# Four mask steps of graph 0 and layer 1's to 3's weights, later in a recorded order

## The chip, the cores and the metric

The kernel runs on one core of a Trainium2 chip. The time is the device time of one execution in microseconds; below, "us" is microseconds. Engines are named as the profile names them: PE is TensorE (PEld its weight loads), DVE is VectorE, ACT is ScalarE, POOL is GpSimd, SP is the engine that issues most of the transfers.

## The reference

Sixteen graphs of 1024 nodes with 256 features each go through four layers. Every layer normalizes the features, takes the positive part and adds its own result to them.

```
x: (16, 1024, 256) f32, adj: (16, 1024, 1024) int32 of 0 and 1, symmetric, ones on the diagonal
for each layer:
    h = max(layernorm(x), 0)
    x = x + layer(h, adj)
layer 0:  Wh = h W; e = leaky_relu(f1_i + f2_j, 0.2), f = Wh a; softmax over axis 1 of e where adj > 0; elu(att Wh)
layer 1:  the same with softmax over the last axis
layer 2:  relu(h W_upd + mean over neighbours of h W_msg + bias)
layer 3:  4 heads of 64: edges by type (adj is 0 or 1, so one type), leaky_relu 0.01, softmax,
          relu(att Wh + bias) + Wh, layernorm with gamma and beta
```

The exponential of a leaky ReLU of a sum is the larger of two products of exponentials, so a 1024 x 1024 matrix of weights comes from one row (the same on all 128 partitions) and one number for each partition.

## The kernel before

A graph's 1024 nodes are eight tiles of 128 (index n, i or j). In layer 0 (`layer0`, L742) a graph goes through these stages:

- *Projection* (L744 to L748): for each of eight tiles, two matmuls into PSUM (`project`, L683, tile ps_proj) and one ACT copy to hs (L746). Then `m.step()` (L747).
- *Row* (L750): the column of one attention term is gathered (L717), transposed on PE (L699, ps_col), exponentiated twice on ACT (L703, e_row), written to DRAM (L705, d_row) and read back as a broadcast to all partitions (L711, row), 512 KB each; layer 0 needs two such rows.
- *j loop* (L766 to L783): for each j, `m.step(2)` while steps are left; DVE makes p from the rows (L769), multiplies it by the mask and sums it (L771), takes the reciprocal (L772); ACT scales hs by it (L773). PE multiplies p by hs for the two output tiles i=0 and i=1 (L759, the "early" tiles; two PSUM buffers).
- *i loop* (L786 to L796): output tiles i=2 to 7, sixteen L759 matmuls each; ACT makes e and v (L791, L793), DVE adds them to the features (L736, L737 in `residual`), after each second tile a shift (L635); ACT makes hn (L667) and a sum of squares (L640), and PE transposes hn (L680, `flip`) for the next layer.

Layer 1 (`layer1`, L798) has the same stages with one row, one DVE instruction for each p (L822) and matmuls at L815.

*Masks.* `Mask` (L548) turns the int32 adjacency into bytes in sixteen steps for a graph, two for each tile j. A step (L575) is an ACT instruction over 128x512 with a sum; it reads a tile raw, of which there are three buffers, and then issues the load of the next raw on SP (L566, 256 KB). Graph 0 has four steps among the statistics at its start (L1011), then one after each projection, and the rest in the j loop. `Mask(1)` issues graph 1's first three loads.

*Weights.* Layer 0's are loaded first. `more()` (L1037) makes the others: `weights01` (L495) loads wx, wts and avs and makes two further columns of wx with PE (L507, ps_wa) and four DVE copies (L511); `weights2` (L513) loads two matrices and four rows (each broadcast to 128 partitions, 128 KB), and adds -2 to row_beta on DVE (L521); `weights3` (L523) loads wx, w3ts and a3s and makes eight columns with eight small products (L534) and sixteen DVE copies (L535, L536). a3s shares its two buffers (tag "e") with the tile e of L791. Each load is held back by a one-element copy (`behind`, L482) that reads the last p tile recorded so far, which makes the load wait until that p is written. The loads of later graphs' features (xs, L545, POOL) and of layer 2's adjacency (adj, L585, POOL) are held back in the same way.

*Order.* All graphs are generators. A queue sorted by a running time (L1050) takes the one that is due, lets it record instructions up to its next `yield`, and adds the yielded number to its time. Graphs start 120 apart. A scheduler then orders each engine's instructions from what was recorded; instructions passed to `later` (all of SP's loads among them) keep the recorded order. Graph 0's j loop is recorded at 26.6 to 47.4, its i loop from 47.4 to 78.6 and layer 1's projections from 80.9.

Of the kernel before, what the change touches and what calls it, by code (L numbers as in the profile page):

```python
# [421 lines left out]
def tile_simple_stack(  # L422
# [12 lines left out]
    B, N, D = x.shape  # L435
# [77 lines left out]
    def weights2():  # L513
        wx[2] = t = load_w(w2_msg, D, "wx2", 2 * D)
        later(nc.sync.dma_start(t[:, :, D:], w2_upd.rearrange("(c p) f -> p c f", p=P)))
        for name, src in (("bias2", bias2), ("bias3", bias3), ("gamma3", gamma3), ("beta3", beta3)):
            rows[name] = const.tile([P, D], F32, name=f"row_{name}")
            behind(rows[name][:1, :1])
            later(nc.sync.dma_start(rows[name], src.partition_broadcast(P)))

        nc.vector.tensor_scalar(rows["beta3"], rows["beta3"], -2.0, None, op0=OP.add)  # L521
# [16 lines left out]
    def load_x(b):  # L538
        t = state.tile([P, NT, D], F32, tag="xs", name="xs", bufs=3)
        if 0 < b < 3:  # L540
            behind(t[:1, 0, :1])
            behind(t[:1, PER, :1])
        for g in range(NHALF):
            part = slice(g * PER, (g + 1) * PER)
            nc.gpsimd.dma_start(t[:, part, :], x[b, g * HALF : (g + 1) * HALF].rearrange("(n p) d -> p n d", p=P))  # L545
        return t
# [136 lines left out]
    def project(norm, w, n, width):  # L683
        ps = mm_ps.tile([P, HALF], F32, tag="mm", name="ps_proj")
        for c in range(DC):
            nc.tensor.matmul(ps[:, :width], norm.ht[:, c, n * P : (n + 1) * P], w[:, c, :width], start=(c == 0), stop=(c == DC - 1))  # L686
        return ps

    def new_hs(name="hs"):
        return state.tile([P, NT, W3], F32, tag="hs", name=name, bufs=3)  # L690

    def spread(col, n, scales, name):

        k = n * NT
        ps = tr_ps.tile([P, P], F32, tag="tr", name="ps_col")
        nc.tensor.transpose(ps[:k, :], col, ident)  # L699
        all_rows = []  # L700
        for scale in scales:
            e = small.tile([H * NT, P], F32, tag="e_row", name="e_row", bufs=2)
            nc.scalar.activation(e[:k, :], ps[:k, :], AF.Exp, scale=scale)  # L703
            d = dram.tile([n, N], F32, tag=f"row_{name}", name="d_row", bufs=4)
            later(nc.sync.dma_start(d.rearrange("r (t p) -> (r t) p", p=P), e[:k, :]))  # L705
            all_rows += [d[r] for r in range(n)]
        return all_rows

    def everywhere(d, tag):
        row = work.tile([P, N], F32, tag=tag, name="row", bufs=2)  # L710
        later(nc.sync.dma_start(row, d.partition_broadcast(P)))  # L711
        return row

    def column(src, n):

        col = small.tile([P, H, NT], F32, tag="col", name="col", bufs=2)
        nc.vector.tensor_copy(col[:, :n, :], src.rearrange("p t n -> p n t"))  # L717
        return col[:, :n, :].rearrange("p n t -> p (n t)")

    def watch(b, layer, terms):  # L720
        k = b * 3 + layer
        nc.vector.tensor_reduce(top[:, k : k + 1], terms, axis=AX.XY, op=OP.max, apply_absolute_value=True)

    def weights(name):
        return work.tile([P, N], F32, tag="p", name=name, bufs=NT)

    def residual(xs, i, v, after, e=None):

        x = xs[:, i, :]
        if i % 2 == 0:  # L730
            if i == NT - 2:
                after.settle()
            after.flip()
            after.sums = small.tile([P, 2], F32, tag="sums", name="sums")
        if e is not None:
            nc.vector.scalar_tensor_tensor(x, e, 1.0, x, op0=OP.min, op1=OP.add)  # L736
        nc.vector.scalar_tensor_tensor(x, v, 0.0, x, op0=OP.max, op1=OP.add, accum_out=after.sums[:, i % 2 : i % 2 + 1])  # L737
        if i % 2:
            after.pair(xs, i // 2, after.sums)


    def layer0(b, xs, m, norm, after):  # L742
        hs = new_hs()
        for n in range(NT):  # L744
            ps = project(norm, wx[0], n, D + 2)
            nc.scalar.activation(hs[:, n, : D + 2], ps[:, : D + 2], AF.Copy, scale=norm.rs[n])  # L746
            m.step()  # L747
            yield 0.9  # L748
        mask = m.bytes
        row_a, row_b = [everywhere(d, "row") for d in spread(column(hs[:, :, D : D + 1], 1), 1, (1.0, S), "l0")]  # L750
        q = small.tile([P, NT], F32, tag="q", name="q")
        nc.scalar.activation(q, hs[:, :, D + 1], AF.Exp, scale=1.0 - S)
        watch(b, 0, hs[:, :, D : D + 2])
        yield 6.38
        ps_ = []
        early = [at_ps.tile([P, HALF], F32, tag="at", name="ps_o0") for _ in range(EARLY)]

        def product(ps, i, j):
            m = nc.tensor.matmul(  # L759
                ps[:, :D], ps_[j][:, i * P : (i + 1) * P], hs[:, j, :D], start=(j == 0), stop=(j == NT - 1)  # L760
            )
            if i < EARLY and j < 7:
                later(m)

        for j in range(NT):
            if m.raws:  # L766
                m.step(2)
            p = weights("p0")
            nc.vector.scalar_tensor_tensor(p, row_a, q[:, j : j + 1], row_b, op0=OP.mult, op1=OP.max)  # L769
            z = small.tile([P, 2], F32, tag="z", name="z", bufs=8)  # L770
            nc.vector.scalar_tensor_tensor(p, p, 1.0, mask[:, j, :], op0=OP.mult, op1=OP.mult, accum_out=z[:, 0:1])  # L771
            nc.vector.reciprocal(z[:, 1:2], z[:, 0:1])  # L772
            nc.scalar.activation(hs[:, j, :D], hs[:, j, :D], AF.Copy, scale=z[:, 1:2])  # L773
            ps_.append(p)
            if b == 0:
                gates.append(p)
            for i, ps in enumerate(early):
                if j:
                    product(ps, i, j - 1)
            yield 2.6  # L780
        for i, ps in enumerate(early):
            product(ps, i, NT - 1)
        for i in range(NT):  # L783
            if i < EARLY:
                ps = early[i]
            else:  # L786
                ps = at_ps.tile([P, HALF], F32, tag="at", name="ps_o0")
                for j in range(NT):
                    product(ps, i, j)
            e = work.tile([P, D], F32, tag="e", name="e")  # L790
            nc.scalar.activation(e, ps[:, :D], AF.Exp)  # L791
            v = work.tile([P, D], F32, tag="v", name="v")
            nc.scalar.copy(v, ps[:, :D])  # L793
            residual(xs, i, v, after, e)
            yield 3.9
# [49 lines left out]
    def degrees(b):  # L845

        t = small.tile([P, NT], F32, tag="deg", name="deg", bufs=2)
        halves = squares[:, b * NT * NHALF : (b + 1) * NT * NHALF].rearrange("p (n g) -> p n g", g=NHALF)
        nc.vector.tensor_tensor(t, halves[:, :, 0], halves[:, :, 1], op=OP.add)
        return t  # L850
# [155 lines left out]
    def graph(b):  # L1006
        xs = loaded.pop(b)
        m = masks.pop(b)
        norm = Norm()
        for g in range(NT // 2):  # L1010
            norm.pair(xs, g)  # L1011
            m.step()
            yield 2.66
        for layer, inputs in ((layer0, (m,)), (layer1, (m.bytes,)), (layer2, ())):
            yield 2.36
            norm.settle()
            norm.flip()
            after = Norm(degrees(b) if layer is layer1 else None)
            yield from layer(b, xs, *inputs, norm, after)
            norm = after  # L1020
        yield 1.44
        norm.flip()
        res = state.tile([P, NT, H, HW], F32, tag="res", name="res", bufs=1)
        hs = yield from layer3(b, xs, m.bytes, norm, res)
        return tail(b, xs, hs, res)
# [3 lines left out]
    def loads(b):  # L1029
        loaded[b] = load_x(b)  # L1030
        yield 30.0
        masks[b] = Mask(b)
        yield 0


    APART = 120.0
    def more():  # L1037

        weights01(1, w1, w1_t, a1, (1, 0))
        yield 21.6  # L1040
        weights2()
        yield 10.0
        weights3()
        yield 0
# [2 lines left out]
    next(loads_0)  # L1047
    weights01(0, w0, w0_t, a0, (0, 1), wait=False)
    next(loads_0)
    queue = [(32, 0, more())] + [(b * APART, b, graph(b)) for b in range(B)] + [(b * APART - 80, b, loads(b)) for b in range(1, B)]  # L1050
    while queue:
        queue.sort(key=lambda g: g[:2])
        at, b, g = queue.pop(0)
# [86 lines left out]
```

## Time and profile before

| | us |
|---|---|
| eight runs, median (lowest to highest) | 2619.87 (2618.07 to 2626.23) |
| the profiled execution: its time | 2620.04 |
| its span, first to last instruction | 2617.7 |
| first p of layer 0 (L769), graph 0 | 35.41 |
| last mask product of layer 0's j loop (L771) starts | 54.91 |
| layer 1's row is issued (L711) | 101.17 |
| first p of layer 1 (L822) | 105.65 |

The page's first rows give each engine's busy time and share of the span; its rows of digits cut the span into 40 slices of 65 us, with the busy share of each in tenths and the granted TensorE clock. The chain of waits follows the work that ended last backward, with the start and length of each piece in us. The timeline lists instructions in order: start, length, engine, line, operation, what it writes from what it reads, and in brackets the engine's idle time before and what ended it. "SPq" and "POOLq" rows are the issue of a transfer, not the transfer. The busy time of the engines in stretches of the first 120 us (from and to, length, then busy us and number of instructions for each engine, the mean granted clock, the share of the DMA engines and GB/s):

```
core 0: us, PE busy (x) PEld busy (x) DVE busy (x) ACT busy (x) POOL busy (x), PEclk, DMA share, GB/s
30.00:35.40 5.40, 0.00 (x0) 0.00 (x0) 0.00 (x0) 0.00 (x0) 0.00 (x0) 0.50 0.77 242
35.40:56.20 20.80, 10.87 (x29) 8.57 (x30) 19.92 (x41) 3.55 (x8) 1.57 (x2) 0.50 0.23 68
56.20:63.20 7.00, 6.70 (x31) 5.51 (x30) 4.09 (x27) 4.03 (x12) 4.79 (x6) 0.96 0.58 175
63.20:73.10 9.90, 9.90 (x50) 8.43 (x48) 2.95 (x11) 4.81 (x15) 1.70 (x3) 1.00 2.13 273
73.10:79.80 6.70, 4.70 (x20) 3.16 (x19) 1.34 (x12) 1.45 (x4) 0.00 (x0) 0.81 0.81 267
79.80:86.00 6.20, 6.20 (x22) 5.26 (x23) 1.38 (x8) 3.27 (x10) 0.00 (x0) 0.66 0.01 3
86.00:99.60 13.60, 12.53 (x58) 9.26 (x56) 2.13 (x9) 8.06 (x22) 1.21 (x2) 1.00 0.00 0
99.60:107.10 7.50, 0.05 (x2) 0.05 (x1) 1.45 (x2) 4.30 (x12) 0.00 (x0) 0.60 0.58 175
107.10:116.60 9.50, 9.46 (x32) 7.37 (x32) 8.38 (x9) 5.60 (x17) 0.00 (x0) 0.78 0.58 194
```

### The profile page before, as it was taken

The numbers are of one execution on the slowest core, as the hardware profiler recorded it, in microseconds if no ns is written. First come the engines' busy times: TensorE is split into PE (matmuls) and PEld (weight loads), VectorE is DVE, ScalarE is ACT, GpSimd is POOL, SyncE is SP. The second block draws the span as 40 slices with busy tenths as digits, with TensorE's granted clock in tenths as the row PEclk, the third lists the DMA queues.
The fourth block names the chain that finished last, engine by engine and source line by source line (L and its number), as shares of the span: only waits on it lengthen the run. The fifth ranks groups of instructions, "written<-read, shape, count | busy, mean of one in ns | idle before, by whom it ended". The sixth has DMA issues, their size and how long they took to land.

```text
span 2617.7 us, 62976 instructions
## 1 busy us (share of the span) xinstructions
PE 2472.8 (94%) x26194; PEld 2098.9 (80%) x26194; DVE 1965.8 (75%) x3815; ACT 1447.8 (55%) x4065; POOL 438.4 (17%) x454
## 2 busy tenths in 40 slices
PE   5899999999999999999999999999999999999985
PEld 4688788888878888788888878888888888878864
DVE  4357778787777977778787777877778787777858
ACT  4563755637565474755637565473755637565350
POOL 1010211203012030211203112030211203111021
PEclk7899999999999999999999999999999999999997
DMA  4541441616217261351616216161351616215021
GB/s 154 116 85 54 104 99 58 126 63 141 70 44 151 67 125 55 96 108 58 125 58 144 72 52 143 66 125 54 98 106 58 125 59 141 72 52 118 26 65 36
DMA packets 212633, 233.76 MB, mean 89 GB/s; under 512 B 10416, under 2 KB 161072, under 8 KB 212336
## 3 DMA queue, kind: packets, MB, share of 16 engines
q0 software_dynamic: 137728, 83.90, 19.3%
q1 hardware_dynamic: 74608, 145.73, 17.1%
q8 instruction: 208, 3.41, 0.5%
q14 instruction: 89, 0.73, 0.1%
HBM read 212.35 MB, written 17.24 MB: 88 GB/s over the span
## 4 chain that ended last, share of the span: by engine, by line
PE 51%; DVE 15%; ACT 14%; DMA 9%; issue 8%; POOL 2%; SPq 0%; DVEq 0%; POOLq 0%; ACTq 0%
PE ps_o L759 16%; PE ps_proj L686 11%; PE ps_o L942 11%; PE ps_o L883 6%; DVE p L929 5%; DVE p L822 5%; ACT hn L667 3%; DMA raw<-in_adj_t 3%; DMA row<-d_row 3%; ACT mask L575 3%; PE pt_h L680 2%; ACT unread L640 2%; PE ps_o L877 2%; PE ps_o L815 2%; POOL rs L593 2%
## 5 line engine op out<-in xcount | busy, mean ns | idle before, releaser
L929 DVE SCALAR_TENSOR_TENSOR p<-row,q,mask 128x1024 f32<-128x1024 f32 x512 | 633.2, 1279 | 61.5 <-PE ps_o L942 50.9
L942 PEld LDWEIGHTS ps_o<-hb,p 128*64 128x64 f32 x16384 | 506.2, 138 | 97.6 <-issue 45.3
L942 PE MATMUL ps_o<-hb,p 128*64 128x65 f32 x16384 | 544.7, 224 | 19.8 <-DVE p L929 6.2
L686 PE MATMUL ps_proj<-wx,ht 128*128 128x258 f32 (+2 forms) x2048 | 518.7, 392 | 6.4 <-ACT hs L746 5.0
L815 PE MATMUL ps_o<-hs,p 128*128 128x257 f32 x2048 | 498.6, 390 | 11.8 <-ACT mask L575 7.5
L759 PE MATMUL ps_o<-hs,p 128*128 128x256 f32 x2048 | 493.8, 386 | 16.5 <-ACT hs L773 16.2
L759 PEld LDWEIGHTS ps_o<-hs,p 128*128 128x128 f32 x2048 | 379.9, 192 | 69.6 <-ACT hs L773 20.7
L686 PEld LDWEIGHTS ps_proj<-wx,ht 128*128 128x128 f32 x2048 | 360.5, 190 | 86.2 <-ACT hs L746 16.0
L815 PEld LDWEIGHTS ps_o<-hs,p 128*128 128x128 f32 x2048 | 373.7, 191 | 68.3 <-ACT mask L575 8.0
L592 POOL TENSOR_SCALAR rs<-mv 128x4 f32<-128x4 f32 (+1 forms) x112 | 33.6, 300 | 1559.7 <-ACT unread L640 1545.0
L736 DVE SCALAR_TENSOR_TENSOR xs<-e,xs 128x256 f32<-128x256 f32 x256 | 108.2, 422 | 233.2 <-ACT e L791 162.4
L593 POOL TENSOR_TENSOR rs<-rs,neg_half 128x4 f32<-128x4 f32 (+2 forms) x144 | 257.3, 1790 | 10.7
L667 ACT ACTIVATE hn<-xs,shift 128x256 f32<-128x256 f32 x384 | 176.7, 500 | 128.1 <-DVE shift L635 127.4
L680 PE MATMUL pt_h<-ident,hn 128*128 128x128 f32 x1024 | 184.0, 285 | 38.7 <-ACT hn L667 37.4
L950 ACT ACTIVATE res<-ps_o 128x260 f32<-128x260 f32 x128 | 48.7, 380 | 300.0 <-PE ps_o L942 299.7
L883 PE MATMUL ps_o<-hi,adj 128*128 128x258 f32 x1024 | 201.1, 320 | 3.4 <-DMA adj<-in_adj 2.6
L680 PEld LDWEIGHTS pt_h<-ident,hn 128*128 128x128 f32 x1024 | 118.8, 142 | 106.0 <-ACT hn L667 85.7
L575 ACT ACTIVATE mask<-raw 128x512 uint8<-128x512 int32 x256 | 160.4, 627 | 70.5 <-DMA raw<-in_adj_t 69.4
L585 POOL DMA_DIRECT2D adj<-in_adj x128 | 114.6, 895 | 485.9 <-PE ps_o L883 456.0
L737 DVE SCALAR_TENSOR_TENSOR xs<-v,xs 128x256 f32<-128x256 f32 x384 | 161.0, 422 | 19.6 <-DVE xs L736 0.5
L769 DVE SCALAR_TENSOR_TENSOR p<-row,q 128x1024 f32<-128x1024 f32 x128 | 160.0, 1271 | 19.4 <-DMA row<-d_row 19.4
L883 PEld LDWEIGHTS ps_o<-hi,adj 128*128 128x128 f32 x1024 | 150.9, 190 | 19.7 <-DMA adj<-in_adj 5.7
(108 smaller groups left out, 3007.7 us busy)
## 6 DMA issues: line engine op xcount, KB each, us to landing
raw<-in_adj_t SPq DMA_DIRECT2D x256, 256.0 KB
adj<-in_adj POOLq DMA_DIRECT2D x128, 512.0 KB, 5.6
row<-d_row SPq DMA_DIRECT2D x112, 512.0 KB
xs<-in_x POOLq DMA_DIRECT2D x32, 512.0 KB, 7.8
out<-xs SPq DMA_DIRECT2D x32, 512.0 KB
wx<-in_w SPq DMA_DIRECT2D x3, 256.0 KB
d_row<-e_row SPq DMA_DIRECT2D x48, 4.0 KB
wts<-in_w_t SPq DMA_DIRECT2D x2, 256.0 KB
```

Of the source, the lines that this page charges most:

```text
L575: nc.scalar.activation(self.bytes[:, n, g * HALF : (g + 1) * HALF], raw, AF.Square, accum_out=squares[:, k : k + 1])
L593: nc.gpsimd.tensor_tensor(rs[:, :n], rs[:, :n], neg_half[:, :n], op=OP.pow)
L667: nc.scalar.activation(hn, xs[:, 2 * g + k, :], AF.Relu, scale=scale, bias=bias)
L680: nc.tensor.transpose(pt[:, c, k * P : (k + 1) * P], hn[:, c * P : (c + 1) * P], ident)
L686: nc.tensor.matmul(ps[:, :width], norm.ht[:, c, n * P : (n + 1) * P], w[:, c, :width], start=(c == 0), stop=(c == DC - 1))
L737: nc.vector.scalar_tensor_tensor(x, v, 0.0, x, op0=OP.max, op1=OP.add, accum_out=after.sums[:, i % 2 : i % 2 + 1])
L759: m = nc.tensor.matmul(ps[:, :D], ps_[j][:, i * P : (i + 1) * P], hs[:, j, :D], start=(j == 0), stop=(j == NT - 1))
L769: nc.vector.scalar_tensor_tensor(p, row_a, q[:, j : j + 1], row_b, op0=OP.mult, op1=OP.max)
L815: nc.tensor.matmul(ps[:, : D + 1], ps_[j][:, i * P : (i + 1) * P], hs[:, j, : D + 1], start=(j == 0), stop=(j == NT - 1))
L883: nc.tensor.matmul(ps[:, : D + 2], adj_n[j][:, i, :], h[:, i, : D + 2], start=False, stop=(h is lo and i == NT - 1), skip_group_check=True,)
L929: nc.vector.scalar_tensor_tensor(p, row, q[:, jj, h : h + 1], mask[:, jj, :], op0=OP.max, op1=OP.mult)
L942: nc.tensor.matmul(pss[g][part, k * HW : (k + 1) * HW], ps_[t][:, i * P : (i + 1) * P][:, part], hbv[:, j + t, h, :], start=(j == 0 and t ...
```

## The change

After the projection's tiles 4 to 7, graph 0 alone no longer makes a mask step; its remaining eight steps, and the four loads that they issue, are recorded in the j loop, behind the row, two for each j. The other graphs are as before. `more()` starts at 60 instead of 32 of the recording queue's time: layer 1's weights at 60 (in the i loop of layer 0, after i=3) instead of 32 (in the j loop), layer 2's at 81.6 instead of 53.6 (now behind the loads of `Mask(1)`, recorded at 70), layer 3's at 91.6 instead of 63.6 (now behind layer 1's row).

```
@@ layer0
             nc.scalar.activation(hs[:, n, : D + 2], ps[:, : D + 2], AF.Copy, scale=norm.rs[n])
-            m.step()
+            if b or n < 4:
+                m.step()
             yield 0.9
@@ the recording queue
-    queue = [(32, 0, more())] + [(b * APART, b, graph(b)) for b in range(B)] + [(b * APART - 80, b, loads(b)) for b in range(1, B)]
+    queue = [(60, 0, more())] + [(b * APART, b, graph(b)) for b in range(B)] + [(b * APART - 80, b, loads(b)) for b in range(1, B)]
```

## The prediction

> **What bounds the kernel now.** I read the page's busy rows first, to see whether a shift made early can be lost again, then the chain of waits and the timeline of the first 120 us.
>
> ```profile
> span 2617.7 us, 62976 instructions
> PE 2472.8 (94%) x26194; PEld 2098.9 (80%) x26194; DVE 1965.8 (75%) x3815; ACT 1447.8 (55%) x4065; POOL 438.4 (17%) x454
> ...
> PE   5899999999999999999999999999999999999985
> ...
> PEclk7899999999999999999999999999999999999997
> ```
>
> TensorE is busy over nine tenths from the third slice on; its idle time lies in the first two slices (0 to 131 us) and at the end. In the built order every engine has the same instructions as before. POOL's order is unchanged; on ACT 98 places in a row differ, on PE 114, on DVE 85, on SP 26, all within graph 0's layers 0 and 1. So the change is worth what TensorE's idle and slow-clock time before about 117 us gains or loses, and the rest moves along.
>
> Where that idle time comes from, by the chain of waits:
>
> ```profile
> 24.80 2.89 DMA raw<-in_adj_t
> 27.71 0.72 ACT mask L575 x2
> 28.44 0.32 ACT e_row L703 x2
> ...
> 46.12 2.86 DMA avs<-in_a
> ...
> 49.11 1.84 PE ps_wa L507 x8
> 50.95 7.78 PE ps_o L759 x22
> ...
> 67.52 0.44 DVE xs L736
> 67.97 7.00 DMA a3s<-in_a
> ...
> 80.72 5.30 PE ps_o L759 x16
> ```
>
> The reader is to see three costs that the edit aims at: the row of exponentials waits behind a mask step, which waits for an adjacency transfer; TensorE waits for layer 1's small vectors (avs); it waits for layer 3's (a3s), 7.00 us after their issue. The timeline tells why a3s is late and what else is queued there:
>
> ```profile
> 58.84 0.38 SPq L519 DMA_DIRECT2D row_beta<-in_beta  x1
> 65.97 0.29 DVE L521 TENSOR_SCALAR row_beta<-row_beta 128x256 f32<-128x256 f32 x1 [4.76 <-DMA row_beta<-in_beta]
> 75.11 0.58 PE L534 MATMUL ps_wa<-a3s,w3ts 64*128 64x10 f32 x4 [2.00 <-DMA a3s<-in_a]
> ```
>
> L521, an addition to a weight row, stands in VectorE's order between the residuals and waits 4.76 us for the last broadcast of layer 2's weights. TensorE has i=3 and i=4 to do meanwhile. This wait is the one to follow.
>
> **Part 1, mask steps behind the row.** Three mask steps (0.63 + 0.19 us each) leave ScalarE between the projections, and the one waiting on its transfer until 27.71 no longer stands ahead of e_row. ps_col ends at 27.81 even with the old projections, so e_row starts at least 0.5 us sooner than 28.34. With the steps gone the last hs follows its projection (TensorE ends those at 26.33) and not 26.73; I take 0.9 us, with 0.5 and 1.0 as ends. SP's queue issues the row pair behind 11 instead of 15 adjacency loads; five now follow it instead of one. The row leads them in the queue, so I add nothing for those; at 101.17 a single row with loads behind landed for a start at 105.65, 4.5 us, against 5.5 us for the pair here, so half a microsecond is the bound. Five masks (11 to 15) now run behind the row; the last that stands ahead of j=0's scaling needs its load by about 39, and a load takes 5.2 us at worst here (issued 30.73, used 35.94), so it is about level with that scaling (40.29 less 0.9). VectorE is the bound there, not ScalarE: no cost.
>
> **Part 2, layer 1's weights out of the j loop.** On VectorE the two gate copies (0.12 us) and the wait with four L511 copies (49.90 to 51.37 less 0.3 for what stays) go: 1.3 us. The last masked product, ended at 56.12, ends at 56.1-0.9-1.3 = 53.9. But the order now puts a statistics instruction (L631) of graph 1 ahead of the last reciprocal. Its data are issued behind a copy that follows the sixth p: about 50.6, and such a transfer took 5.0 us (median of the two issued at 51.68); 4.7 for the first half. So L631 waits till 55.3, and the last reciprocal comes at 55.8 against 56.19: most of the 2.2 us is given back. Without that wait it would be 54.2.
>
> TensorE then has tile 0 ready at 57.3 instead of 58.7, but loses its run-up: now it works without a gap from 50.8 and the granted clock goes from 0.50 to 1.00 at 56.7 (windows: 0.50 in 54 to 56, 0.82 in 56 to 58). After the change it waits between the last j's, and I take one step of the clock later (the steps in this trace lie 3.4 us apart): 60.1. A matmul takes 0.43 us at half clock and 3.47/16 = 0.217 at full. i=3 ends at 66.7 against 67.05: -0.35, with -1.9 (no L631 wait, clock kept) and +0.7 as ends. Then the eight ps_wa matmuls of layer 1 come, 1.84 us at half clock, 1.0 at full, and i=4 (3.5) ends at 71.2 against 70.5.
>
> **Part 3, the queue behind.** SP now issues, from about 56.0: layer 1's weights (512 KB), graph 1's three adjacency loads (768 KB), layer 2's weights (512 KB), four row broadcasts (512 KB). row_beta, last of them, has 1.28 MB more ahead than before. POOL's adj loads (2 MB) are gated by copies that stay at 58.5 and move no earlier.
>
> ```profile
> DMA packets 2128, 1.45 MB, mean 241 GB/s; under 512 B 71, under 2 KB 2076, under 8 KB 2128
> ## 3 DMA queue, kind: packets, MB, share of 16 engines
> q0 software_dynamic: 1617, 0.82, 100.1%
> q1 hardware_dynamic: 511, 0.63, 42.3%
> ```
>
> That is 62 to 68 us: with POOL's queue (q0) running, SP's (q1) moves 0.63 MB in 6 us, 0.105 MB a us. Alone it took 0.52 MB in 46 to 48, and 1.57 MB in 12 to 20 (0.2 a us, adjacency). So by 62.2, when q0's data begin, layer 1's weights and some 0.44 MB of adjacency have gone; 1.35 MB remain, 12.9 us at 0.105: 75. With half a us of receipt row_beta lands at 75.5. Ends: 70, at the lone rate (w2 2.1 us after 63.8, rows 4.1 us), and 79, if q0's xs transfers take a larger share.
>
> The Trainium skill, "DMA: Bandwidth & Descriptors", section Queues, rings and completion order, says that each DMA engine takes its queues in turn, a whole packet from each. If that meant equal counts of the packets shown above, rows of 1 KB would get two thirds against 0.5 KB pieces, 0.16 MB a us, and land at about 71; the time would be some 2617. The trace shows three packets of q0 for one of q1, so the measured rate stands.
>
> VectorE reaches L521 at 68.5, and behind it stand i=3's last residual, the shift, ScalarE's hn and so the transposes (L680) that TensorE has ahead of i=5. From landing to the end of those transposes: 0.3 + 0.5 + 0.2 + 0.9 + 0.5 = 2.4 us, so i=5 starts at 77.9, and TensorE has idled from 71.2 for nearly 6 us. Its clock will have dropped (after the wait from 73.1 it was 0.50 in 78 to 84 here). i=5 then takes six matmuls to 80.6 and ten at full clock, to 82.7; i=6 ends at 86.2, against 86.02. If the clock comes one step later, 87.9. I take 86.6: +0.6. So the gain of moving layer 3's weights away (from 73.1 to 86.02 for what is 22 matmuls, 4.8 us: 8.1 us) is eaten by the wait at L521.
>
> **Part 4, layer 3's weights into layer 1.** Their three loads are issued behind layer 1's row, at 101.2; 1.03 MB had moved by 106 in before's same place, so a3s lands near row + 1.5 us and TensorE, busy with j=0 till 3.2 us after the first p, hardly waits. VectorE bounds this stage (L822, eight in 9.66 us) and gets 16 copies, 0.45 us for four in a run (75.51 to 75.96): 1.8, and 0.5 of waiting for the first group's matmuls. +2.3 us, with 1.0 (copies in gaps) and 4.5 (a3s 7.0 us after issue, as before, and TensorE's 16 small matmuls at half clock, 0.25 each) as ends. ScalarE's masks of graph 1 start 2 us later here; the eight ahead of e ended 1.9 us before e, and e moves too: no cost.
>
> **Sum.** +0.6 + 2.3 = +2.9 us on the profiled execution's 2620.0 (span 2617.7 and 2.3 around it): 2622.9. The median of the runs is 2619.9, so 2623 by either.
>
> **Rivals.** *Row_beta in time.* If it lands by 69, nothing waits at L521 and the clock stays: i=4 at 71.2, transposes 0.44, two tiles of 3.47: 78.6 instead of 86.0, -7.4 + 2.3 = -5.1, 2614.9. For it: SP's queue alone moves 0.2 to 0.26 MB a us. Against: 1.28 MB more ahead, and q0 starts at 62.
>
> *Row_beta later still.* At 79, i=5 starts at 81.4; the clock is up at 84.0 at best: six matmuls slow, ten fast, 86.2; i=6 89.7: +3.7 + 2.3 = +6.0, 2626. It passes +5.2 from a landing near 78. For it: the queues moved 0.241 MB a us in all over 56 to 80, 5.79 MB, to the very end at 80, and SP's last transfer now is the one waited for. Against: it leads xs in time.
>
> *Layer 3's weights are hidden in layer 1*, TensorE's cold start there covering the copies: +1.0 instead of 2.3, 2621.6.
>
> **How the numbers follow.** What a measurement of this kernel can tell from no change is about 0.2%, 5.2 us. My forecast 0.50 (2620.5 to 2625), hidden layer 3 0.12, row in time 0.09, row later 0.29. Faster takes most of the early row, 0.08; slower most of the late one and a tail of part 4, 0.30; same 0.62. The range runs from 2616.1 (row_beta at 70: i=5 from 72.4 at full clock, i=6 at 79.8, -6.2 + 2.3) to 2628.2 (row_beta at 79 and part 4 at its upper end, +3.7 + 4.5).
>
> **What would show it.** L521 with an idle time of 5 to 9 us ending near 75; TensorE idle from 71 to 77 ahead of L680; L631 waiting for xs ahead of the last reciprocal; sixteen L535 and L536 copies between the L822; e_row near 27.4. L521 without a wait, or a shift of layer 1's row (101.17) by more than 4 us either way, would make the prediction wrong.

## The result, and the profile after

The changed kernel takes 2626.48 us (median of 12 runs, 2622.36 to 2637.48) against 2620.12 (34 runs, 2616.45 to 2626.23): a ratio of 1.0026, with a 95% interval of 1.0018 to 1.0033. That is 6.8 us more, 4.7 to 8.6. The time lies inside the predicted range, but the prediction's own figure was 2.9 us and "no change", and the measured value is just past the 0.2% that it set as the bound. The profiled execution took 2626.91 us against 2620.04.

From L748 on, lines stand one further than in the kernel before: the p of layer 1 is L823 (was L822), its matmuls L816 (was L815). Lines of the weights (L521, L534 to L536) and of `residual` (L736, L737) are as before. The page's first rows:

```profile
span 2624.7 us, 62970 instructions
...
PE 2476.4 (94%) x26194; PEld 2097.9 (80%) x26194; DVE 1966.6 (75%) x3815; ACT 1449.4 (55%) x4065; POOL 438.7 (17%) x454
...
PE   5899999999999999999999999999999999999985
...
PEclk8899999999999999999999999999999999999997
```

At this scale nothing differs: the same work, PE at nine tenths from the third slice, a first slice with a better clock (8 for 7). What changed lies in the first 125 us. The chain of waits there (start, length, piece):

```profile
28.52 0.43 ACT e_row L703 x2
...
51.89 4.38 DMA xs<-in_x
56.29 0.43 DVE st L631
...
64.55 8.13 DMA row_beta<-in_beta
72.70 0.04 DVE row_beta L521
...
72.91 0.44 DVE xs L737 x2
...
73.58 0.52 ACT hn L667
...
74.14 0.84 PE pt_h L680 x4
74.98 8.60 PE ps_o L760 x32
...
98.74 4.30 DMA row<-d_row
...
103.17 1.29 DVE p L823
...
104.60 2.05 PE ps_o L816 x4
106.65 0.95 PE ps_wa L534 x4
107.60 1.16 PE ps_o L816 x2
108.76 0.96 PE ps_wa L534 x4
109.72 2.01 PE ps_o L816 x4
```

The wait for a3s (7.00 us before) and the one for avs are gone. In their place the chain goes over L521's wait for row_beta, as predicted. The rest was not foreseen in this form: in layer 1's j loop TensorE, over which the chain runs, alternates between layer 1's products (ps_o) and layer 3's small ones (ps_wa). The timeline shows L521's wait from both sides, on VectorE and on TensorE (the idle time before each instruction is in brackets):

```profile
72.70 0.29 DVE L521 TENSOR_SCALAR row_beta<-row_beta 128x256 f32<-128x256 f32 x1 [3.67 <-DMA row_beta<-in_beta]
...
74.14 0.84 PE L680 MATMUL pt_h<-ident,hn 128*128 128x128 f32 x4 [2.13 <-ACT hn L667]
```

Three marks make the account: the third projection's copy to hs (L746), layer 1's first p, and the first reciprocal of a share (`shares`, end of the j loop's two early tiles). Before:

```profile
21.90 0.48 ACT L746 ACTIVATE hs<-ps_proj,rs 128x258 f32<-128x258 f32 x1
...
105.65 9.66 DVE L822 SCALAR_TENSOR_TENSOR p<-row,q,mask 128x1024 f32<-128x1024 f32 x8 [6.37 <-DMA row<-d_row]
...
116.16 0.17 DVE L836 RECIPROCAL shares<-ps_o 128x1 f32<-128x1 f32 x1 [0.86 <-PE ps_o L815]
```

And after (the first p is in the chain above, at 103.17):

```profile
22.91 0.48 ACT L746 ACTIVATE hs<-ps_proj,rs 128x258 f32<-128x258 f32 x1
...
120.72 0.17 DVE L837 RECIPROCAL shares<-ps_o 128x1 f32<-128x1 f32 x1 [0.86 <-PE ps_o L816]
```

The copy comes ahead of everything that the change moves; it stands at 21.90 us before and at 22.91 after, so all the times after are to be read 1.0 us earlier. Counted from that copy, layer 1's first p comes at 83.75 before (105.65 - 21.90) and at 80.26 after: 3.5 us gained. From the first p to the first reciprocal of a share it is 10.51 us before and 17.55 after: 7.0 us lost. The sum, 3.5 us, is the change's account in these two profiles.

### The profile page after: what moved, and what is told of

Same layout as the page of the kernel before. It is cut to its first block, busy times and chain, and to the rows that moved or that the text cites. A ratio compares the mean times of both kernels' runs of the same rounds, so it can differ in the third digit from the quotient of the medians.

```text
span 2624.7 us, 62970 instructions
## 1 busy us (share of the span) xinstructions
PE 2476.4 (94%) x26194; PEld 2097.9 (80%) x26194; DVE 1966.6 (75%) x3815; ACT 1449.4 (55%) x4065; POOL 438.7 (17%) x454
## 4 chain that ended last, share of the span: by engine, by line
PE 49%; ACT 15%; DVE 14%; DMA 10%; issue 8%; POOL 2%; SPq 0%; DVEq 0%; POOLq 0%; ACTq 0%
PE ps_o L760 16%; PE ps_proj L686 11%; PE ps_o L943 10%; PE ps_o L884 6%; DVE p L930 5%; DVE p L823 4%; DMA raw<-in_adj_t 3%; ACT hn L667 3%; DMA row<-d_row 3%; ACT mask L575 3%; PE pt_h L680 2%; PE ps_o L816 2%; ACT unread L640 2%; PE ps_o L878 2%; POOL rs L593 2%
## 5 line engine op out<-in xcount | busy, mean ns | idle before, releaser
L930 DVE SCALAR_TENSOR_TENSOR p<-row,q,mask 128x1024 f32<-128x1024 f32 x512 | 633.3, 1279 | 62.2 <-PE ps_o L943 50.8
L816 PE MATMUL ps_o<-hs,p 128*128 128x257 f32 x2048 | 502.2, 391 | 12.6 <-DVE p L823 11.0
L816 PEld LDWEIGHTS ps_o<-hs,p 128*128 128x128 f32 x2048 | 373.3, 191 | 69.3 <-issue 8.5
L736 DVE SCALAR_TENSOR_TENSOR xs<-e,xs 128x256 f32<-128x256 f32 x256 | 108.2, 423 | 238.6 <-ACT e L792 166.7
L737 DVE SCALAR_TENSOR_TENSOR xs<-v,xs 128x256 f32<-128x256 f32 x384 | 161.0, 422 | 19.3 <-DVE xs L736 0.5
L884 PEld LDWEIGHTS ps_o<-hi,adj 128*128 128x128 f32 x1024 | 151.0, 190 | 20.5 <-DMA adj<-in_adj 5.8
```

The costliest lines, as they stand in the source:

```text
L816: nc.tensor.matmul(ps[:, : D + 1], ps_[j][:, i * P : (i + 1) * P], hs[:, j, : D + 1], start=(j == 0), stop=(j == NT - 1))
L884: nc.tensor.matmul(ps[:, : D + 2], adj_n[j][:, i, :], h[:, i, : D + 2], start=False, stop=(h is lo and i == NT - 1), skip_group_check=True,)
L930: nc.vector.scalar_tensor_tensor(p, row, q[:, jj, h : h + 1], mask[:, jj, :], op0=OP.max, op1=OP.mult)
```

## The experiments

Each ratio is against the kernel before, run on the same chip at the same time. Behind the first comparison there were three such groups of runs, each on a chip of its own; in them that kernel's median was 2629.91, 2629.04 and 2628.97 us, 9 us above the 2620.12 of the comparison above, so only ratios are compared between groups. "First p" and "L521" count from the third projection's copy; "stage" is from layer 1's first p to its first share reciprocal; "half clock" is the length of the stretch of granted clock 0.50 that holds the stage's beginning (or, where the clock was kept up until then, the one that follows).

| kernel | ratio, 95% interval | L521 runs at | first p | stage | half clock |
|---|---|---|---|---|---|
| before | | 44.1 | 83.8 | 10.51 | 10.2 |
| before_again | one run, 2627.89 us | 46.0 | 87.4 | 10.78 | 10.2 |
| after | 1.0026 (1.0018 to 1.0033) | 49.8 | 80.3 | 17.55 | 17.1 |
| after_again | 1.0020 (1.0010 to 1.0030) | 50.0 | 80.2 | 19.85 | 23.9 |
| e1_masks_only | 0.9992 (0.9981 to 1.0004) | 45.1 | 87.7 | 10.73 | 10.2 |
| e2_weights_only | 1.0009 (0.9998 to 1.0019) | 51.9 | 82.0 | 19.56 | 20.5 |
| e3_w3_before_row | 0.9984 (0.9973 to 0.9996) | 51.3 | 83.3 | 10.51 | 10.2 |
| e4_beta_late | 0.9995 (0.9986 to 1.0005) | 91.7 | 76.0 | 16.40 | 13.7 |
| e8_warm | 1.0005 (0.9993 to 1.0017) | 50.4 | 81.4 | 19.16 | 17.1 |
| e7_w3_row_beta | 0.9973 (0.9962 to 0.9985) | 86.8 | 76.9 | 10.51 | 10.2 |
| e12_one_tile | 0.9998 (0.9988 to 1.0007) | 50.8 | 81.3 | 15.76 | 17.1 |
| e5_few_copies | 1.0007 (0.9998 to 1.0017) | 50.4 | 81.6 | 15.91 | 17.1 |
| e6_before_beta_late | 0.9993 (0.9982 to 1.0004) | 94.7 | 84.8 | 10.51 | 10.2 |
| e10_cures_masks_back | 0.9970 (0.9959 to 0.9981) | 87.7 | 77.9 | 10.51 | 10.2 |

The kernel before, profiled twice, differs by 3.6 us at the first p, so single profiles place the account to 3 or 4 us; the stage's length repeats far better in the kernels with a short one (10.51 to 10.78 in seven profiles).

### The two halves of the change: e1_masks_only, e2_weights_only

The mask steps alone, on the kernel before:

```
-            m.step()
+            if b or n < 4:
+                m.step()
```

> The mask steps behind the row alone, the weights where they were. Theory: e_row 0.8 us sooner after the third hs of the projection than before (6.4 us there), the rest of layer 0 moves along, ratio 0.9997 (-0.8 us), which the runs can't tell from 1. Rival (the four masks ahead of the first scaling hold ScalarE and TensorE): first e of the i loop later than before, ratio above 1.0005.

Layer 1's first p stands at 87.7 beside 87.4 of before_again, on the same chip, and the ratio can't be told from 1. The row's exponentials come 6.65 us after the mark: 0.5 us sooner than in before_again (7.18), but no sooner than in the first profile of the kernel before (6.44). L521 still waits, 5.53 us here. The weights alone (the changed kernel with a plain `m.step()`):

> The later start of the weights alone, mask steps where they were. Theory (the weights carry the whole change: layer 3's products inside layer 1's j loop cost 7 us there, the removed waits of layer 0 give back 2 to 3): 2626.5 + 0.8, since only the row's 0.8 us is lost again, so 2627 and a ratio near 1.0027; the stretch from layer 1's first p to its first share is 17 to 18 us, as in the changed kernel (17.6), against 10.5 before. Rival (the mask steps behind the row are the cost, by holding ScalarE or the queue): 2620 or less and the stretch near 10.5.

The stage is 19.56 us, the half clock 20.5: the loss belongs to the weights, whatever the masks do. The ratio, 1.0009, is below the 1.0027 that was expected and that of the whole change in two other groups of runs (1.0026, 1.0020); with intervals of a thousandth either way this doesn't make the masks a loss, but they are no measured gain.

### The loss in layer 1: e3_w3_before_row

Layer 3's weights come 2.6 earlier in the recorded order, so that their small products fall into TensorE's wait for layer 1's row instead of into its j loop:

```
         weights2()
-        yield 10.0
+        yield 7.4
         weights3()
```

> The changed kernel, with layer 3's weights recorded just ahead of layer 1's row (at 89 instead of 91.6), so that its loads are ahead of the row in SP's queue and its products and copies fall into the time in which TensorE waits for the row. Theory (the 7 us lie in the products' place inside the j loop): the stretch from the first p to the first share falls from 17.6 to 10.5 or 11 us, layer 1's row comes about 1 us later (four small products and four copies ahead of the column), the time is 2626.5 - 6 = 2620 to 2621. Rival (the cost comes from the masks or from layer 2's weights and the wait at the row_beta addition): the stretch stays above 15 us or the time above 2625.

The stage is back at 10.51 us, to the hundredth that of the kernel before, with L521's wait still in place (VectorE idle for 5.35 us before it). The ratio falls below 1. So the eight small products and sixteen copies, placed among layer 1's p, were what lost the 7 us. The first p comes 3.0 us later than in the changed kernel (83.3 for 80.3) where 1 was expected; 1.5 us of it stands at L521 already (51.3 for 49.8).

### The wait in layer 0: e4_beta_late, and its control in the kernel before: e6_before_beta_late

L521 is taken out of `weights2` and its addition made with a -2 computed from graph 0's last p of layer 1, so that it can't come before:

```
-    gates = []
+    gates, late = [], []
...
-        nc.vector.tensor_scalar(rows["beta3"], rows["beta3"], -2.0, None, op0=OP.add)
...
+            if b == 0:
+                late.append(p)
...
         weights3()
+        yield 30.0
+        minus2 = const.tile([P, 1], F32, name="minus2")
+        nc.vector.tensor_scalar(minus2, late[-1][:, :1], 0.0, -2.0, op0=OP.mult, op1=OP.add)
+        nc.vector.tensor_scalar(rows["beta3"], rows["beta3"], minus2[:, 0:1], None, op0=OP.add)
```

> The changed kernel, with the addition to row_beta made dependent on layer 1's last p of graph 0, so that it stands behind the j loop of layer 1 in VectorE's order and no residual waits for the load. Theory (the addition's wait held the transposes and through the idle time the clock): TensorE has no idle time near 72 (2.1 us in the changed kernel) and full clock through 75 to 78 (3.4 us at half, worth 1.7), so layer 1's row is issued 3 to 4 us earlier and the time is about 2623. Rival (the wait was hidden: TensorE had other work or the next wait takes its place): row time and total unchanged, 2626 to 2627.

The first p comes 4.3 us sooner than in the changed kernel (76.0 for 80.3) and the clock doesn't fall near 75 us any more; on the chain i=4 (68.50 to 72.06 us), the transposes (0.44) and i=5 and i=6 (6.91) follow one another without a gap. The stage stays long, 16.40. The same edit on the kernel before (with 50.0 for the 30.0):

> The kernel before, with the addition to row_beta (its line 521) moved behind layer 1's last p, and nothing else. Theory (in the kernel before its wait of 4.76 us is covered, since TensorE has i=3 and i=4 to do and the load of a3s, 7.00 us behind the residual of i=3, holds TensorE longer): the chain still holds a wait for a3s of about 7 us, layer 1's first p comes 83 to 85 us after the third projection's start as before (83.7), ratio 0.9993 to 1.0007. Rival (the wait is paid in the kernel before as well, so that the gain of the kernel with both cures owes nothing to the change): a3s issued 1.5 to 4 us sooner, first p 80 to 82 us after that start, ratio 0.9985 to 0.9992.

There it is worth nothing that can be told: the first p stays at 84.8 and the chain still waits for a3s.

```profile
69.64 7.79 DMA a3s<-in_a
...
77.57 0.58 PE ps_wa L533 x4
```

So L521's wait of 4.76 us in the kernel before was covered, as the prediction had it, and became a price only once the change took the a3s load away from behind it.

### Both cures: e7_w3_row_beta, and the masks put back: e10_cures_masks_back

> Both cures in the changed kernel: layer 3's weights recorded just ahead of layer 1's row, and the addition to row_beta behind layer 1's j loop. Theory (the two costs are separate and add): row and first p 4 us earlier than in the changed kernel less 1 for the small products ahead of the column, the stretch 10.5, so the first share comes near 111 us instead of 116.2 before and 120.7 after; 5 us faster than before, ratio near 0.998. Rival (another wait takes the place of either): first share at 115 or later and a ratio of 1.000.

This version beats both kernels: 0.9973, 7.1 us under the kernel before (3.9 to 10.0). Its account against the first profile is about as much: first p at 76.9 (6.9 us less than before), stage 10.51; against before_again, profiled on the same chip, it is 10.5 us less and 0.3. The small products cost about 0.9 us in their new place by two single profiles (first p 76.9 against 76.0 in e4_beta_late). They run behind the last projections and ahead of ps_col:

```profile
91.01 0.33 PE ps_wa L533 x2
...
91.73 0.37 PE ps_wa L533 x2
...
92.52 0.34 PE ps_wa L533 x2
92.86 0.22 PE ps_col L698
```

Between 91.01 and 92.86 there are gaps in which VectorE copies, and the row starts that much later; on a clock that is still full the products are done in passing. With the mask steps back at all eight projections:

> The kernel with both cures (layer 3's products in the row's wait, the addition to row_beta behind layer 1), but with graph 0's mask steps at all eight projections as in the kernel before. Theory (the mask steps behind the row are worth the 0.8 us that the row's exponentials gain, on top of the cures): e_row 6.4 to 7.2 us after the third projection's start instead of 5.7, layer 1's first p 77.5 to 78.5 us after it instead of 76.9, ratio 0.9973 to 0.9981. Rival (the masks in the j loop take the 0.8 us back, since graph 1's statistics wait there for their data): first p at 76.9 again, ratio 0.9970 to 0.9974. The two ratios touch, so the stage's times decide.

The stage's times go as the theory said (the first exponentials of the row 6.6 us after the mark instead of 5.7; first p 77.9 instead of 76.9), but the ratio is 0.9970 against 0.9973. Two profiles are no proof of 1.0 us, and the times show none: what the masks are worth stays below what was measured.

### Why the small products cost so much: e8_warm, e12_one_tile, e5_few_copies

The first guess was the cold clock at the stage's start. Fifteen products whose results are not used were put on TensorE while it waits for layer 1's row:

```
         row = everywhere(d_row, "row")
+        if b == 0:
+            for _ in range(15):
+                ps = hd_ps.tile([P, HALF], F32, tag="hd", name="ps_warm")
+                nc.tensor.matmul(ps[:, :D], norm.ht[:, 0, N - P :], wx[1][:, 0, :D], start=True, stop=True)
```

> The changed kernel with 15 more products of 128x256, whose results nobody reads, in graph 0 while TensorE waits for layer 1's row, so that its clock is not let down before the j loop. Nothing else is touched: copies and order as in the changed kernel. Theory A (the 7 us come from the half clock, which lasts 17 us here because the small products break up the run that would raise it): granted clock 1.00 through the j loop, the stretch from first p to first share falls from 17.6 to 12.5 or 13 us, the time to about 2622. Theory B (VectorE's sixteen copies and the two PSUM buffers are what costs, at any clock): the stretch stays above 16 us, the time 2626.

The clock was full when the stage began and the stage was still 19.16 us. But the clock fell 2.4 us behind the first p, so this run doesn't show the stage at full clock. What happened is in the stretches, first of all engines and then of L534 alone (from and to, length, PE busy, PEld busy, and further on the mean granted clock):

```profile
102.00:105.40 3.40, 0.93 (x4) 0.68 (x4) 2.36 (x2) 0.00 (x0) 0.00 (x0) 1.00 1.06 267
105.40:108.80 3.40, 3.37 (x10) 2.29 (x10) 2.48 (x7) 2.04 (x6) 0.00 (x0) 0.50 0.42 148
108.80:112.20 3.40, 3.40 (x11) 2.41 (x9) 2.07 (x6) 1.86 (x5) 0.00 (x0) 0.50 0.67 231
...
105.40:108.80 3.40, 1.03 (x4) 0.93 (x4) 0.50 0.42 148
108.80:112.20 3.40, 1.02 (x4) 0.93 (x4) 0.50 0.67 231
```

The 15 products were over at 101.6 and the first ps_o came at 104.47, so one stretch of 3.4 us was only 0.93 us busy; the clock fell at its end, 105.4. Then TensorE's rows are full, 3.4 of 3.4 us, in five stretches one after another, and the clock stays at 0.50 for 17.1 us. 1.02 us of each of the first four, 30%, are small products of ten columns.

Is it the copies, or the alternation, that does this? e12_one_tile puts the four small products of a half into one PSUM tile, so that they need not wait for copies and all run in a row; the sixteen copies stay, eight behind each half's products. e5_few_copies, shown here, does the same with two copies instead of sixteen.

```
         for fc in range(DC):
+            ps = mm_ps.tile([P, HALF], F32, tag="mm", name="ps_wa3")
             for h in range(H):
-                ps = mm_ps.tile([P, HALF], F32, tag="mm", name="ps_wa3")
-                nc.tensor.matmul(ps[:, :T2], w3ts[:, h, fc * P : (fc + 1) * P], a3s[:, h, :], start=True, stop=True)
-                nc.vector.tensor_copy(t[:, fc, D + h : D + h + 1], ps[:, 0:1])
-                nc.vector.tensor_copy(t[:, fc, D + H + h : D + H + h + 1], ps[:, T : T + 1])
+                nc.tensor.matmul(
+                    ps[:, h * T2 : (h + 1) * T2], w3ts[:, h, fc * P : (fc + 1) * P], a3s[:, h, :],
+                    start=(h == 0), stop=(h == H - 1), skip_group_check=True,
+                )
+            nc.vector.tensor_copy(
+                t[:, fc, D:].rearrange("p (k h) -> p k h", k=2),
+                ps[:, : H * T2].rearrange("p (h k t) -> p k h t", k=2, t=T)[:, :, :, 0],
+            )
```

> The changed kernel, but the four small products of a half of layer 3's weights go to one PSUM tile, so that all eight can run in a row on TensorE without waiting for copies; VectorE still makes the sixteen copies. In the changed kernel the stage from layer 1's first p to its first share reciprocal took 17.55 and 19.85 us (10.5 before), at half clock for 17 to 24 us. Theory (the small products are broken into short runs that wait for copies, this keeps the clock at half, and TensorE sets the pace): with one run the clock comes back as in the kernel before, half clock 10 to 14 us around this stage, and only the copies' time on VectorE is left, 1.8 to 2.3 us: stage 12.3 to 13.5, ratio to before 0.9990 to 1.0008. Rival (sixteen copies on the engine that sets the pace, with what waits for them, are the cost however the products are grouped): stage 16 to 20, half clock 17 us or more, ratio 1.0018 or more.

> As the kernel with one PSUM tile for each half, and the eight columns of a half are copied by one instruction: two copies instead of sixteen. Theory (broken runs and clock): stage 10.5 to 12, that is 1.5 to 2 us less than with sixteen copies from the same tiles, half clock 10 to 14 us, ratio to before 0.9985 to 1.0003. Rival (layer 3's small products cost by their own time and the wait for a3s, not by runs or copies): stage 14 or more and no difference over 0.5 us between two and sixteen copies.

The theory of the broken runs fell. The stage is 15.76 us with sixteen copies (between the two expectations, while the ratio lies in the theory's stretch) and 15.91 with two (the rival's side), and half clock lasts 17.1 us in both. Sixteen copies or two make no difference that can be told, so the copies on VectorE are not the cost. Ending the alternation took 1.6 to 1.8 us off the changed kernel's 17.55 and 3.9 to 4.1 off its repetition's 19.85, and the ratios, 0.9998 and 1.0007, stand below 1.0020 and 1.0026; but most of the loss is still there. And e4_beta_late, which keeps the alternation, has a stage of 16.40 with 13.7 us of half clock, so what the alternation costs isn't told apart from when the clock steps. The chain of e12_one_tile has the whole stage in three pieces of TensorE:

```profile
105.51 2.05 PE ps_o L820 x4
107.56 3.52 PE ps_wa L534 x16
111.08 8.74 PE ps_o L820 x26
```

Before, the same 30 records of ps_o took 9.06 us, and the chain went over them, not over VectorE's p:

```profile
107.08 9.06 PE ps_o L815 x30
```

Here they take 2.05 + 8.74 = 10.79, and the small products 3.52, 0.22 us for each of their 16 records (two for a product), at half clock: 5.25 us together, the stage's whole growth. In the changed kernel the small products on the chain sum to 3.6 us and the 30 records of ps_o to 12.3: 3.6 + 3.2 and 0.2 of gaps, the 7.0 us. The stretches of the changed kernel, again all engines and then L534 alone:

```profile
105.60:109.10 3.50, 3.50 (x11) 2.16 (x10) 2.88 (x7) 2.04 (x6) 0.00 (x0) 0.50 0.50 168
109.10:112.50 3.40, 3.40 (x10) 2.50 (x11) 1.85 (x7) 2.04 (x6) 0.00 (x0) 0.50 0.68 227
112.50:115.90 3.40, 3.40 (x9) 1.88 (x8) 1.44 (x4) 1.57 (x6) 0.00 (x0) 0.51 0.68 232
115.90:119.30 3.40, 3.30 (x15) 2.41 (x15) 2.27 (x6) 0.00 (x0) 0.00 (x0) 1.00 0.27 92
...
105.60:109.10 3.50, 1.44 (x6) 1.34 (x7) 0.50 0.50 168
109.10:112.50 3.40, 1.22 (x5) 1.01 (x5) 0.50 0.68 227
112.50:115.90 3.40, 0.62 (x3) 0.52 (x3) 0.51 0.68 232
```

And of the kernel before, in the same place:

```profile
107.90:111.30 3.40, 3.40 (x9) 2.66 (x9) 3.40 (x4) 1.32 (x5) 0.00 (x0) 0.50 0.71 232
111.30:116.20 4.90, 4.90 (x23) 4.00 (x22) 4.04 (x5) 3.25 (x10) 0.00 (x0) 1.00 0.62 212
```

Before, one stretch full of ps_o and the clock is back. After, small products take 41%, 36% and 18% of three stretches, and the clock is back only behind the third. At half clock TensorE needs 2.05 us for a j where VectorE needs 1.27 for a p, so it is TensorE that sets the pace until then; VectorE's busy time falls from 3.40 of 3.40 us to 1.44.

### The two kernels again: before_again, after_again

> The kernel before, for a profile beside the others of this call. Expected as on record: first p of layer 1 near 105.7, stretch to the first share 10.5 us, one wait of TensorE for a3s near 73. If its stretch or its waits differ by more than 2 us from the first profile, the first 120 us vary from run to run by that much and single profiles can't settle smaller sums.

> The changed kernel once more, beside the others of this call. Theory: the stretch from layer 1's first p to its first share again 17 to 20 us, ratio 1.001 to 1.003. Rival (the first profile was a chance of the clock's phase): the stretch differs by more than 4 us from 17.6.

Side by side on one chip the stage took 10.78 and 19.85 us and the ratio was 1.0020 (1.0010 to 1.0030): the loss repeats.

## Why the prediction was right or wrong

Times of the changed kernel are taken 1.0 us back here, as said above.

*Masks behind the row (-0.9).* Right for the row: its first exponentials come 5.61 us after the mark instead of 6.44, 0.83 us sooner. By itself, in e1_masks_only, the step gave 0.5 us against before_again; in both of those profiles the granted clock was 0.50 for 3.4 us from about 22.5, which it was not in the first two. As predicted, part of it is lost again, and no run measured a gain from the masks.

*Layer 1's weights out of the j loop (-0.35 at i=3).* Right, step by step. L631 waits for xs and starts at 55.3 (predicted 55.3), the last reciprocal comes at 55.6 (55.8), i=3 ends at 66.7 (66.7), and TensorE falls idle at 71.0 (71.2).

*The queue behind (+0.6).* Right in its mechanism, wrong in its size and so in its sign. L521 waits, i=5 waits for L521, the clock falls. But row_beta landed near 71.7, not 75.5 (L521 idle 3.67 us, not 5 to 9), and i=5 and i=6 then took 8.6 us, as long as predicted (8.7). i=6 ended at 82.6, not 86.6. The term that was off is the rate of SP's queue beside POOL's, 0.105 MB a us, taken from the kernel before. In the changed kernel, over the same 62 to 68 us:

```profile
DMA packets 2406, 1.73 MB, mean 289 GB/s; under 512 B 77, under 2 KB 2260, under 8 KB 2406
...
q0 software_dynamic: 1580, 0.80, 68.8%
q1 hardware_dynamic: 826, 0.93, 56.1%
```

SP's queue (q1) moved 0.93 MB in 6 us, 0.155 MB a us, two packets of q0 for one of its own where it had been three; over 66 to 72 it was 0.74 MB, 0.123 a us. In the kernel before the queue wasn't idle in that stretch: over 62 to 65.9, up to row_beta's landing, it moved 0.40 MB, again 0.103 a us. What differed is what it carried: row broadcasts and what follows them there, the adjacency and the matrices of layer 2 first here. That the kind of load sets the share fits, but no run tried it alone. The prediction weighed and set aside an estimate from the rule of the Trainium skill ("DMA: Bandwidth & Descriptors", Queues, rings and completion order), read as equal counts of packets: 0.16 MB a us and a landing at 71. That is nearer to the measured rate and landing than the row that was preferred, but in part by chance: the counts were 1580 and 826, not equal, and two thirds of the 289 GB/s moved here would have been 0.19 MB a us.

*Layer 3's weights in layer 1 (+2.3).* This is the term that failed: 7.0 us, beyond its upper end of 4.5. The prediction charged the copies to VectorE (1.8) because VectorE bounds the stage, and named the small products at half clock only in the upper end. The runs show the reverse: sixteen copies or two cost the same within 0.2 us, the small products at half clock cost 3.5 to 3.6, and the clock, which comes back later, another 1.7 to 3.2. What was missing is that the stage's bound is VectorE only at full clock; the chain of the kernel before had TensorE's ps_o there for 9.06 of the 10.51 us. The rival that these weights are hidden falls by the same numbers.

*Sum.* -3.5 and +7.0 make +3.5, beside a predicted +2.9: the two errors, -4.1 and +4.7, cancel. That the time came close to 2622.9 at all is luck. The measured differences are 6.8 (4.7 to 8.6) and 5.3 us (2.6 to 7.9). The second pair of profiles, before_again and after_again, makes -7.1 and +9.1, so +1.9: both accounts lie some 3 us below the measured difference. In the two first profiles the distance between the same VectorE instructions is 4.6 us behind the stage, the start's 1.0 among it, wanders between 2.9 and 5.4 up to 1440 us and is 7.2 at the end. Two profiles of the kernel before drift against each other by nearly as much (6.1 near 130 us, 8.3 at the end), so the 3 us between account and median can't be given a place, and stay open.

*Chances.* The time was in the range, though not in the forecast's own stretch (2620.5 to 2625), but "same" got 0.62 because the row's uncertainty was put at 4 us and part 4's at 3. The rivals held one mechanism for slower, row_beta still later, which did not happen, so that its 2626 is near the measured time by chance; the slower outcome came from the part whose upper end was worked out in half a sentence.

## What to carry to other kernels

Work moved into a stage is priced on each of its engines, and at the clock that the stage starts with, not only on the engine that bounds it: a stage that VectorE paces at full clock was paced by TensorE at half, and small products that cost 0.9 us in a wait of TensorE cost 5 to 9 us among its first products after one. A wait that is covered (L521) becomes the next price when its cover is removed, so the cover and the wait are to be moved together: here that turned a loss of 0.2 to 0.3% into a gain of 0.3%. The rate of a queue beside another one, read from one stretch, was off by half in the next kernel (0.103 against 0.155 MB a us); a forecast that hangs on it needs both ends priced.

## What the runs showed of the hardware

- TensorE's rows can be full and the granted clock stay at half: in e8_warm for 17.1 us, of which four stretches of 3.4 us had 30% in products of ten columns. Full stretches with 23 to 83% of them (two each of e12_one_tile, e5_few_copies and the changed kernel) didn't bring the clock back either; two with 18% (one of the changed kernel, one of e4_beta_late) and those with none did. Nor did stretches without small products that TensorE filled to 70 to 80% (after_again, 40.9 to 51.2 us: 2.58 and 2.38 of 3.40, 2.60 of 3.50), while 3.27 of 3.40 in the next one did. So by these rows the small products count towards the clock about as idle time does.
- The fall of the clock says the same. In e7_w3_row_beta TensorE was busy for 2.43 of 3.40 us, 2.30 of them with the small products, and the clock fell at the end; in e2_weights_only 1.85 of 3.40 us in wider products (96.7 to 100.1) held it for the next stretch.

```profile
91.20:94.60 3.40, 2.43 (x17) 2.01 (x16) 1.80 (x18) 2.26 (x8) 0.00 (x0) 1.00 0.01 1
94.60:98.00 3.40, 0.00 (x0) 0.00 (x0) 0.05 (x1) 1.96 (x5) 0.00 (x0) 0.50 0.53 170
```

- That it is their width, ten columns, fits all of these, but no run tried it by itself, as with products of other widths in the same place. The Trainium skill, "TensorE: Matmul & The Clock Gate", section What's actually happening, has the clock return after one busy window of some 3.4 us; the steps seen here lie 3.4 us apart, but one full window by the profile's rows was not enough.
- The clock fell again within one stretch of 3.4 us that was 0.93 us busy (e8_warm, 102.0 to 105.4), right after 3.03 us of work in the stretch before.
- Before any changed instruction, the third projection's copy stood anywhere between 21.6 and 24.1 us in fourteen profiles, and the medians of the kernel before were 2620 us in the first comparison and 2629 in the three others. Neither has to do with the change; the second is larger than the effects sought here, the first a good part of them.
